# Layer 0 of a four-layer network: products of two slots together in even slots, two convolution taps together in odd slots

## The chip, the cores and the metric

The kernel runs on one core of one Trainium2 chip. The metric is the time of the device in microseconds for one launch, all four layers included. A core has five engines that work side by side and wait for each other through semaphores: PE (TensorE: matrix products and transposes), DVE (VectorE), ACT (ScalarE), POOL (GpSimd) and SP (SyncE, which here issues most DMAs). PEld is PE's weight load, which can overlap its products.

## The reference, cut to what matters

Each of four layers adds the output of one block to `x`, an array of 4 images of 64 x 64 tokens with 128 channels in float32. The change touches layer 0 alone, a selective scan in four directions over the tokens:

```python
xz = x @ in_proj_w.T
xh, z = jnp.split(xz, 2, axis=-1)
z = silu(z)
xc = silu(depthwise_conv_3x3(xh) + conv_b)          # 256 channels
xs = stack([x0, x1, x0[..., ::-1], x1[..., ::-1]])  # rows, columns, and both backwards
dts, Bm, Cm = split(einsum(xs, x_proj_weight))
delta = softplus(dts @ dt_projs_weight + bias)
h = exp(delta * A) * h + (delta * u) * B            # for each of 16 states n, token by token
y = einsum('bkdn,bkn->bkd', h, C)                   # sum over the 16 states
y = layernorm(sum_over_directions(y + Ds * xs)) * z
return y @ out_proj_w.T
```

Here `u` is the input of one direction. The scan over `h` runs along 4096 tokens for 256 channels, 16 states, 4 directions and 4 images.

## The kernel before, in words

**Units and slots.** Layer 0 walks through 128 units: an image `b` (4), a direction `k` (4) and a chunk `c` of 512 tokens (8). A unit has 16 slots `n`, one for each state; there are 2048 slots. The order of instructions on PE, ACT, DVE and POOL is written out by hand: each engine executes in the order in which the loop emits.

**One slot.** POOL multiplies `dB = du * B` (L684). For each half `s` of the channels ACT computes `dA = exp(delta * A)` into a PSUM bank (L689, three banks in turn) and DVE runs the scan `h` (L690) over 512 tokens. The states of four slots form a group `G` of one tile `h`. Some slots later (`LAG`, and the place in a queue) `transposed()` takes a quarter of a group: PE transposes eight 128 x 128 blocks into `pt` (L538; one buffer of two PSUM banks), and ACT copies `pt` to the tile `hT` (L548).

**Products.** `products()` multiplies a copied `hT` with `W`, a sparse arrangement of C that sums over the states, into the PSUM tiles `yT` (L573): four products with 32 output rows each in every slot, which the profile shows as eight records. In a direction `k == 0` four products with the diagonal `D_diag` (L562) stand ahead of them. When a group is the last of its unit, `yT` is added to `y`, and the result is stored. `products()` is called in the slot after that in which its `hT` was copied: after the transposes of that slot, before the slot's side work.

**Side work.** Generators, wrapped in `Side`, give out the work for other images in pieces, each with a kind: `l` (loads), `m`, `n`, `x`, `z` (gates), `f`, `g` and `c` (a tap of the convolution). A piece may be placed in the slots that `SIDE` lists for its kind, and `due()` paces the pieces evenly by their number. A convolution is nine taps (L159), each a product of 128 x 128 weights with 512 tokens that PE makes in two records, added up in one PSUM bank `cv`. Its first tap is placed at `n == 11`; then the property `inside` makes the loop give a tap in each of the next eight slots, so it ends at `n == 3` of the next unit. The bank `m`, of which there is one, is shared by all side work and by the projections of the next unit: `xd_ps` at n=6, `dp` (L465) at n=7 and n=9. `limited` (L474) is DVE's clamp of `delta`, which reads `dp` at n=9 and n=11. After a convolution ACT and DVE compute silu (`e`, in three steps at ACT) and ACT copies it by columns (`xw`, L369).

The side work after an image (`after`) normalises `y`, transposes it, writes it scaled to `yg`, multiplies `yg` by the gates on POOL (L411) and projects it on PE.

There are 52 convolutions in the slots: 20 while image 0 is scanned, 16 each with images 1 and 2, none with image 3.

Of the kernel before, what the change touches and what calls it, by code (L numbers as in the profile page):

```python
# [11 lines left out]
F32 = mybir.dt.float32  # L12
# [70 lines left out]
def layer0(sh, A, x_in, x_out, scr, ahead):  # L83
# [7 lines left out]
    with ExitStack() as ctx:  # L91
# [60 lines left out]
        def conv(xn, s, bank):  # L152

            for t in range(9):
                yield "c"
                if t == 0:
                    pm = bank("cv")
                dy, dx = divmod(t, 3)
                nc.tensor.matmul(  # L159
                    pm,  # L160
                    lhsT=taps[:, s, t, :],
                    rhs=xn[:, dy : dy + 8, dx : dx + 64],
                    start=(t == 0),
                    stop=(t == 8),
                )
            return pm
# [207 lines left out]
        def after(b, st, later, bands):  # L374

            for c in bands:
                yield "l"
                rows = slice(c * CH, (c + 1) * CH)
                if kept:
                    y = kept.pop()  # L380
                else:
                    y = tmp.tile([P, 4, 2 * P], F32, name="yf", tag="t4", bufs=4)
                    nc.sync.dma_start(y, tiles(scr(f"y2{b % 2}")[rows, :]))
                z = tmp.tile([P, 2, CH], F32, name="zf", tag="t4", bufs=4)
                nc.sync.dma_start(z, scr(f"z{b % 3}")[:, :, rows].rearrange("s p t -> p s t"))
                mv = small.tile([P, 4, 2], F32, name="ln_mv")
                for q in range(4):
                    nc.vector.bn_aggr(mv[:, q, :], st[:, 4 * c + q])

                rs = small.tile([P, 4], F32, name="ln_r")  # L390
                later("act1", nc.scalar.activation, rs, mv[:, :, 1], AF.Ln, bias=sh.eps5)
                yield "n"

                nb = spare("nb")[:, 0:4]
                nc.scalar.activation(nb, rs, AF.Exp, scale=-0.5)
                for q in range(4):
                    later("dve", normed, y[:, q, :], mv[:, q, 0:1], nb[:, q : q + 1])
                yg = tmp.tile([P, 2, CH], F32, name="yg", bufs=2)
                for s in range(2):
                    yield "m"  # L400
                    pt = spare("pg")
                    for q in range(4):
                        nc.tensor.transpose(pt[:, q * P : (q + 1) * P], y[:, q, s * P : (s + 1) * P], sh.ident)
                    norm = dict(scale=on_w[:, s : s + 1], bias=on_b[:, s : s + 1])
                    later("act0", nc.scalar.activation, yg[:, s, :], pt, AF.Identity, **norm)
                yield "f"
                xr = tmp.tile([P, 4, DM], F32, name="xr", tag="t2", bufs=4)
                nc.sync.dma_start(xr, tiles(x_in(b)[rows, :]))
                if b < NB - 1:
                    yield "g"  # L410
                nc.gpsimd.tensor_tensor(yg, yg, z, ALU.mult)  # L411
                yield "m"
                op = spare("op").rearrange("p (q d) -> p q d", q=4)
                for q in range(4):
                    for s in range(2):
                        nc.tensor.matmul(
                            op[:, q, :], lhsT=yg[:, s, q * P : (q + 1) * P], rhs=w_out[:, s, :], start=(s == 0), stop=(s == 1)
                        )
                later("dve", residual, b, rows, xr, op, slots=2)
# [100 lines left out]

        LAG = 7
        queue = []
        copied = None

        def transposed():

            nonlocal copied
            todo, copied = copied, None
            pt = None
            if queue:  # L530
                G = queue[0]
                q = G["q"]
                G["q"] += 1
                pt = ps.tile([P, 4, 2, P], F32, name="pt")
                for j in range(4):
                    t0 = q * P + j * 32
                    for s in range(2):
                        nc.tensor.transpose(  # L538
                            pt[:, j, s, :], G["h"][:, s, t0 : t0 + 32, :].rearrange("p t n -> p (t n)"), sh.ident
                        )  # L540
                if q == 3:
                    queue.pop(0)
            if todo is not None:
                products(*todo)
            if pt is not None:
                hT = tmp.tile([P, 4, 2 * P], F32, name="hT")
                copied = G, q, hT
                return lambda: nc.scalar.copy(hT, pt.rearrange("p j s d -> p j (s d)"))  # L548
            return lambda: None

        def products(G, q, hT):
            U = G["unit"]
            rev = U["rev"]
            qo = 3 - q if rev else q
            e = qo // 2
            if U["yT"][e] is None:
                U["yT"][e] = psy.tile([P, 2, 2 * P], F32, name=f"yT{e}")
                if U["k"] == 0:
                    for r in range(2):
                        for s in range(2):  # L560
                            t0 = (2 * e + r) * P
                            nc.tensor.matmul(  # L562
                                U["yT"][e][:, r, s * P : (s + 1) * P],
                                lhsT=U["u"][:, s, t0 : t0 + P],
                                rhs=D_diag[:, s, :],
                                start=(r == 0 and s == 0),
                                stop=False,
                                skip_group_check=True,
                            )
                    U["started"] |= {(e, j) for j in range(4)}  # L570
            for j in range(4):
                jo = 3 - j if rev else j
                nc.tensor.matmul(  # L573
                    U["yT"][e][32 * jo : 32 * jo + 32, qo % 2, :],
                    lhsT=U["Ws"][G["g"]][:, :, 4 * q + j],
                    rhs=hT[:, j, :],
                    start=((e, jo) not in U["started"]),
                    stop=(G["g"] == 3),
                    skip_group_check=True,
                )  # L580
                U["started"].add((e, jo))
            if G["g"] == 3 and q % 2:

                y, k = U["y"], U["k"]
                ye = y[:, 2 * e : 2 * e + 2, :]
                if U["pos"] == 0:
                    (nc.vector.tensor_copy if q == 3 else nc.scalar.copy)(ye, U["yT"][e])
                else:
                    nc.vector.tensor_tensor(ye, ye, U["yT"][e], ALU.add)
                if k == 2:  # L590
                    for r in range(2):
                        nc.vector.bn_stats(U["st"][:, 4 * U["pc"] + 2 * e + r, 0, :], y[:, 2 * e + r, :])
                if q == 3 and U["last"]:
                    kept.append(y)
                elif q == 3:
                    nc.sync.dma_start(U["dst"](k), y)
# [45 lines left out]
        with tc.manual_schedule(engines=order):  # L642
            idle = lambda: None
            left = opening(any_bank, [idle, fetched, idle, begun, grown_steps, readied])
            u, ready, bd, Wd, Bb = (got[n] for n in ("u", "ready", "bd", "Wd", "Bb"))
            sides.append(Side(rest(left, spare, later), 18 * len(left), 0, 2 * NS * len(left)))
            for i, (b, k, c) in enumerate(units):
                if i % per == 0:
                    ln_st = small.tile([P, NJ, 1, 6], F32, name="ln_st")
                    first = len(left) if b == 0 else 0  # L650
                    if b + 1 < NB:
                        sides.insert(len(sides) if b == 0 else 0, Side(before(b + 1, spare, later), 17 + 8 * 22, NS * (i + first), (28 - first) * NS))
                rev = k >= 2
                pos = orders[b].index(k)
                pc = NCH - 1 - c if rev else c
# [16 lines left out]
                for n in range(NS):  # L672
# [14 lines left out]
                    for s in range(2):  # L687
# [4 lines left out]
                        )  # L692
                        steps(n, f"act{s}")
                        flush(f"act{s}")
                    copy = transposed() if slot >= LAG else (lambda: None)
                    copy()
                    steps(n, "act2")
                    flush("act2")
# [26 lines left out]

                    inside = [d for d in sides if d.inside]
                    free = not inside and slot >= taken
                    for d in inside or [d for d in sides if free and n in SIDE[d.need] and d.due(slot)][:1]:
                        taken = slot + SPACE[d.need]
                        d.free_at = slot + 1  # L730
                        d.step()
# [40 lines left out]
class Side:  # L772
# [7 lines left out]
    @property  # L780
    def inside(self):

        return self.need == "c" and self.run % 9 > 0

    def due(self, slot):
        wait = self.need == "l" and self.loads and slot < self.loads[0]
# [1404 lines left out]
```

## Time and profile before

| | |
|---|---|
| time, median of 3 runs | 7696.86 us (7693.64 to 7699.71) |
| the profiled execution | 7694.64 us, span 7692.9 us |
| slots of layer 0 | from 112.8 to 5645.7 us of the span |
| busy over the whole span | PE 82%, DVE 88%, ACT 79%, POOL 74% |
| mean granted TensorE clock | 0.965 of full speed |

The profile shows one execution. Times are microseconds from the start of the span unless marked ns. A group's row gives line, engine, operation, the tiles written and read, the shapes and how often it ran, then the time it kept its engine busy, the mean ns of one, and the engine's idle time just before it with what ended most of it. Rows of a timeline give start, duration, engine, line and operation, with equal neighbours merged ("x8"). PE's records overlap their neighbours, so distances there are read from start to start. "pt(n)", "hT(n)" and so on stand for the instruction of that name in slot n.

### The profile page before, as it was taken

How to read it: one execution, taken by the hardware profiler on the slowest of the kernel's cores; microseconds unless marked ns; L12 is line 12 of the kernel's file. 1: busy time of each engine (PE TensorE's matmuls, PEld its weight loads, DVE VectorE, ACT ScalarE, POOL GpSimd, SP SyncE). 2: the span in 40 equal slices, each digit the busy share in tenths (PEclk: the TensorE clock that was granted, in tenths of full speed). 3: DMA queues.
4: the chain of work that ended last, by engine and by line, in shares of the span. 5: the costliest groups of instructions: out<-in, count | busy, mean ns of one | idle time of the engine just before them, and what ended most of it. 6: DMA issues, size and time to landing. Idle time of an engine off the chain costs nothing.

```text
span 7692.9 us, 140985 instructions
## 1 busy us (share of the span) xinstructions
PE 6324.7 (82%) x52796; PEld 3997.2 (52%) x52796; DVE 6751.7 (88%) x8113; ACT 6094.9 (79%) x9683; POOL 5694.2 (74%) x2718
## 2 busy tenths in 40 slices
PE   7888888888889877888887777787789978676789
PEld 3544444444455544445554444454467756564566
DVE  7999999999999999999999999999966655656678
ACT  7999999999999999999999999999843323314667
POOL 4999999999999999999999999999930024123233
PEclk8999999999999999999999999999999978788899
DMA  6555556555656655465565445555532241231332
GB/s 173 171 169 177 176 171 180 168 172 166 189 174 182 189 188 171 155 183 184 174 193 185 166 168 180 176 182 180 176 107 67 63 115 52 77 103 41 103 97 81
DMA packets 1325856, 1158.87 MB, mean 151 GB/s; under 512 B 694134, under 2 KB 1119698, under 8 KB 1258227
## 3 DMA queue, kind: packets, MB, share of 16 engines
q1 hardware_dynamic: 1320898, 1147.43, 48.7%
q8 instruction: 416, 6.82, 0.4%
q10 hardware_dynamic: 4272, 2.43, 0.1%
q14 instruction: 270, 2.20, 0.1%
HBM read 956.37 MB, written 189.21 MB: 149 GB/s over the span
## 4 chain that ended last, share of the span: by engine, by line
PE 34%; ACT 31%; DVE 19%; issue 8%; POOL 4%; DMA 2%; SPq 1%; ACTq 0%; DVEq 0%; POOLq 0%
ACT hT L548 12%; DVE h L690 12%; ACT dA L689 12%; PE pt L538 7%; PE cv L159 5%; PE yT L573 4%; POOL dB L684 3%; ACT e L631 2%; PE pf L917 2%; PE po L930 1%; ACT delta L468 1%; PE pt L1870 1%; PE pu L1161 1%; PE pa L1161 1%; PE pb L1161 1%
## 5 line engine op out<-in xcount | busy, mean ns | idle before, releaser
L690 DVE TENSOR_TENSOR_SCAN h<-dA,state,dB 128x512 f32<-128x512 f32 x4096 | 4921.4, 1268 | 127.0 <-POOL dB L684 48.0
L684 POOL TENSOR_TENSOR dB<-du,Bb 128x1024 f32<-128x1024 f32 x2048 | 4816.6, 2391 | 162.2 <-DVE h L690 121.9
L538 PE MATMUL pt<-ident,h 128*128 128x128 f32 x16384 | 2221.1, 279 | 824.8 <-ACT hT L548 809.6
L689 ACT ACTIVATE dA<-delta,A_neg 128x512 f32<-128x512 f32 x4096 | 2750.0, 695 | 118.3 <-DVE h L690 95.8
L538 PEld LDWEIGHTS pt<-ident,h 128*128 128x128 f32 x16384 | 1810.0, 142 | 1866.0 <-ACT hT L548 1642.5
L548 ACT COPY hT<-pt 128x1024 f32<-128x1024 f32 x2048 | 2077.2, 1014 | 178.6 <-PE pt L538 158.6
L573 PE MATMUL yT<-hT,W 128*32 128x256 f32 x16384 | 1380.2, 409 | 0.3
L573 PEld LDWEIGHTS yT<-hT,W 128*32 128x32 f32 x16384 | 455.8, 150 | 342.6 <-issue 330.2
L159 PE MATMUL cv<-xn,taps 128*128 128x512 f32 x936 | 526.9, 644 | 2.9 <-DVE delta L474 2.9
L1161 POOL TENSOR_TENSOR xg<-xg,so 128x1024 f32<-128x1024 f32 x16 | 39.3, 2467 | 620.0 <-PE pu L1161 619.4
L1908 POOL TENSOR_TENSOR S<-S,sm 128x784 f32<-128x784 f32 x128 | 191.4, 1495 | 414.6 <-DVE sm L1906 243.1
L477 POOL TENSOR_TENSOR du<-delta,u 128x512 f32<-128x512 f32 x256 | 329.2, 1286 | 188.7 <-DVE delta L474 172.3
L465 PE MATMUL dp<-xd,w_dt 65*128 65x512 f32 x512 | 288.7, 646 | 65.7 <-ACT Ct L456 43.8
L448 PE MATMUL xd_ps<-u,w_x 128*48 128x512 f32 x512 | 249.4, 610 | 18.8 <-DVE e L358 17.6
L1915 ACT ACTIVATE S<-S,mx 128x196 f32<-128x196 f32 x512 | 228.0, 449 | 32.2 <-DVE mx L1942 29.8
L159 PEld LDWEIGHTS cv<-xn,taps 128*128 128x128 f32 x936 | 139.2, 188 | 180.6 <-issue 163.2
L918 ACT ACTIVATE h<-pf,b 128x512 f32<-128x512 f32 x128 | 87.7, 687 | 118.8 <-PE pf L917 100.7
L474 DVE SCALAR_TENSOR_TENSOR delta<-delta,dp 128x512 f32<-128x512 f32 x256 | 171.2, 669 | 3.9 <-ACT delta L471 0.8
L1161 POOL TENSOR_TENSOR WX<-wr,Xs 128x544 f32<-128x544 f32 x40 | 60.7, 1517 | 152.2 <-issue 62.9
L1870 PE MATMUL pt<-ident,S 128*98 128x128 f32 x1024 | 166.3, 287 | 3.4 <-POOL S L1908 2.0
L1161 DVE TENSOR_TENSOR WX<-wr,Xs 128x544 f32<-128x544 f32 x88 | 74.1, 860 | 104.4 <-PE pz L1161 59.5
L465 PEld LDWEIGHTS dp<-xd,w_dt 65*128 65x128 f32 x512 | 76.5, 188 | 170.7 <-ACT Ct L456 97.4
(377 smaller groups left out, 7101.9 us busy)
## 6 DMA issues: line engine op xcount, KB each, us to landing
Bb<-l_B SPq DMA_DIRECT2D x512, 1024.0 KB
W<-l_W SPq DMA_DIRECT2D x512, 256.0 KB
l_y<-y SPq DMA_DIRECT2D x127, 512.0 KB
u<-l_xr SPq DMA_DIRECT2D x64, 512.0 KB
u<-l_xw SPq DMA_DIRECT2D x64, 512.0 KB
y<-l_y SPq DMA_DIRECT2D x56, 512.0 KB
V<-l_v SPq DMA_DIRECT2D x512, 49.0 KB
y<-l_y SPq DMA_DIRECT2D x80, 256.0 KB
```

Of the source, the lines that this page charges most:

```text
L159: nc.tensor.matmul(pm, lhsT=taps[:, s, t, :], rhs=xn[:, dy : dy + 8, dx : dx + 64], start=(t == 0), stop=(t == 8),)
L448: nc.tensor.matmul(bank["x"], lhsT=w_x[:, s, k, :], rhs=u[:, s, :], start=(s == 0), stop=(s == 1))
L465: nc.tensor.matmul(bank[s], lhsT=w_dt[:, k, s * P : (s + 1) * P], rhs=xd, start=True, stop=True)
L477: nc.gpsimd.tensor_tensor(du[:, s, :], delta[:, s, :], u[:, s, :], ALU.mult)
L538: nc.tensor.transpose(pt[:, j, s, :], G["h"][:, s, t0 : t0 + 32, :].rearrange("p t n -> p (t n)"), sh.ident)
L548: return lambda: nc.scalar.copy(hT, pt.rearrange("p j s d -> p j (s d)"))
L573: nc.tensor.matmul(U["yT"][e][32 * jo : 32 * jo + 32, qo % 2, :], lhsT=U["Ws"][G["g"]][:, :, 4 * q + j], rhs=hT[:, j, :], start=((e, jo) n ...
L684: nc.gpsimd.tensor_tensor(dB, du, B_now[:, q : q + 1, :].to_broadcast([P, 2, CH]), ALU.mult)
L689: nc.scalar.activation(dA, delta[:, s, :], AF.Exp, scale=A_neg[:, k, s, n : n + 1])
L690: nc.vector.tensor_tensor_scan(h[:, s, :, q], dA, dB[:, s, :], state[:, s, n : n + 1], ALU.mult, ALU.add)
L1161: r = f(*args, **kw)
L1870: nc.tensor.transpose(pt[:, half, hp, :], U["S"][:, e, hp, 98 * half : 98 * half + 98], sh.ident)
```

## The change

Taps go in pairs, and products in even slots:

- `conv` asks for a new piece only before every second tap, so a convolution is five pieces: taps 0 and 1, 2 and 3, 4 and 5, 6 and 7, and 8. Inside a convolution the loop gives a piece only in slots with odd `n`: 11, 13, 15, 1, 3.
- In slots n = 1, 3, 11, 13 and 15 `transposed(hold=True)` calls no products; the `hT` that are waiting are kept in a list, and the next slot makes the products of both. This is so in every unit, with or without a convolution.
- `hT` gets three buffers instead of two, and `yg` one instead of two; each buffer is 4 KB per partition.
- The numbers of pieces by which side work is paced become 10 instead of 18, and 14 instead of 22.

```diff
         def conv(xn, s, bank):
             for t in range(9):
-                yield "c"
+                if t % 2 == 0:
+                    yield "c"
                 if t == 0:
                     pm = bank("cv")
...
-                yg = tmp.tile([P, 2, CH], F32, name="yg", bufs=2)
+                yg = tmp.tile([P, 2, CH], F32, name="yg", bufs=1)
...
-        copied = None
-
-        def transposed():
-
-            nonlocal copied
-            todo, copied = copied, None
+        copied = []
+
+        def transposed(hold=False):
+
+            todo, copied[:] = copied[:], []
             pt = None
             if queue:
...
-            if todo is not None:
-                products(*todo)
+            if hold:
+                copied[:] = todo
+            else:
+                for each in todo:
+                    products(*each)
             if pt is not None:
-                hT = tmp.tile([P, 4, 2 * P], F32, name="hT")
-                copied = G, q, hT
+                hT = tmp.tile([P, 4, 2 * P], F32, name="hT", bufs=3)
+                copied.append((G, q, hT))
                 return lambda: nc.scalar.copy(hT, pt.rearrange("p j s d -> p j (s d)"))
...
-            sides.append(Side(rest(left, spare, later), 18 * len(left), 0, 2 * NS * len(left)))
+            sides.append(Side(rest(left, spare, later), 10 * len(left), 0, 2 * NS * len(left)))
...
-                        sides.insert(len(sides) if b == 0 else 0, Side(before(b + 1, spare, later), 17 + 8 * 22, NS * (i + first), (28 - first) * NS))
+                        sides.insert(len(sides) if b == 0 else 0, Side(before(b + 1, spare, later), 17 + 8 * 14, NS * (i + first), (28 - first) * NS))
...
-                    copy = transposed() if slot >= LAG else (lambda: None)
+                    copy = transposed(n in {1, 3, 11, 13, 15}) if slot >= LAG else (lambda: None)
...
-                    for d in inside or [d for d in sides if free and n in SIDE[d.need] and d.due(slot)][:1]:
+                    for d in [d for d in inside if n % 2] or [d for d in sides if free and n in SIDE[d.need] and d.due(slot)][:1]:
...
-        return self.need == "c" and self.run % 9 > 0
+        return self.need == "c" and self.run % 5 > 0
```

## The prediction

> **What bounds the kernel now.** I read the page first, then layer 0 alone (a row of the windows view), then DVE's waits, then the order of time inside one unit.
>
> ```profile
> span 7692.9 us, 140985 instructions
> L690 DVE TENSOR_TENSOR_SCAN h<-dA,state,dB 128x512 f32<-128x512 f32 x4096 | 4921.4, 1268 | 127.0 <-POOL dB L684 48.0
> ```
>
> ```profile
> 112.00:5646.00 5534.00, 4572.09 (x36175) 2704.32 (x36176) 5388.46 (x5178) 5165.13 (x7415) 5188.49 (x2375) 0.99 0.56 176
> ```
>
> The columns are PE, PEld, DVE, ACT, POOL. In the 5534 us of layer 0's slots DVE is busy 5388: it bounds them, and the scans are 4921.4/2048 = 2.40 us of each slot. The change adds and removes nothing on DVE, so it can win at most the 145 us in which DVE idles. Adding up DVE's idle gaps by slot number, 43.5 us fall in slot n=5 of the 128 units, and 42.0 of these in the 52 units in which a convolution has just ended: about 0.83 us each in 49 of them, 0.37 to 0.42 in three. One such unit, in its order of time (slots 2 to 5; start, duration, engine, line):
>
> ```profile
> 2421.88 1.04 PE L538 MATMUL pt<-ident,h 128*128 128x128 f32 x8
> 2422.84 0.67 PE L573 MATMUL yT<-hT,W 128*32 128x256 f32 x8
> 2423.01 1.01 ACT L548 COPY hT<-pt 128x1024 f32<-128x1024 f32 x1 [0.31 <-PE pt L538]
> 2423.44 1.13 PE L159 MATMUL cv<-xn,taps 128*128 128x512 f32 x2
> 2424.41 1.04 PE L538 MATMUL pt<-ident,h 128*128 128x128 f32 x8
> ...
> 2429.75 0.70 ACT L689 ACTIVATE dA<-delta,A_neg 128x512 f32<-128x512 f32 x1
> ...
> 2430.55 1.30 DVE L690 TENSOR_TENSOR_SCAN h<-dA,state,dB 128x512 f32<-128x512 f32 x1 [0.82 <-ACT dA L689]
> ```
>
> Start to start, PE spends 0.96 on eight transposes, 0.60 on the products, 0.97 on a tap: 2.53 a slot, more than DVE's 2.40. So in the nine tap slots PE leads: ACT's copy hT waits 0.31 for pt, the next dA stands behind that copy, and DVE's lead is used up (at n=3 the scan starts 0.10 after its dA in 49 of 52 cases). At n=4 ACT has two pieces of silu besides, and DVE waits at n=5.
>
> Without a tap PE does not lead:
>
> ```profile
> 728.22 1.09 PE L538 MATMUL pt<-ident,h 128*128 128x128 f32 x8 [0.97 <-ACT hT L548]
> 729.25 0.67 PE L573 MATMUL yT<-hT,W 128*32 128x256 f32 x8
> 730.47 1.09 PE L538 MATMUL pt<-ident,h 128*128 128x128 f32 x8 [0.56 <-ACT hT L548]
> ```
>
> pt has one buffer, so a slot is the round trip pt, hT, pt: 2.25 here. Where the weights were loaded ahead it is 1.12 (2424.41 to the copy at 2425.53) + 1.01 copy + 0.06 = 2.20.
>
> **What the skill's pages say.** "TensorEngine Tiling (Array Packing)", Key Properties, says that a change of tiling mode drains TensorE, not a change of tile. The products use 128x32 tiles, transposes and taps the whole array. The trace agrees and prices it:
>
> ```profile
> 2401.35 1.09 PE L538 MATMUL pt<-ident,h 128*128 128x128 f32 x8
> 2402.28 1.06 PE L562 MATMUL yT<-D_diag,u 128*128 128x128 f32 x8
> ```
>
> ```profile
> 40.60 7.89 PE L159 MATMUL yT<-xn,taps 128*128 128x512 f32 x18
> 48.38 1.12 PE L240 MATMUL pv<-h,w_in 128*128 128x512 f32 x2
> ```
>
> pt to another whole-array group takes 0.93 (2401.35 to 2402.28), where pt to the products takes 1.03 (728.22 to 729.25), both with weights not loaded ahead. Nine taps in a row take 7.78, 0.86 each, against 0.97 behind products. A switch is thus about 0.1 us. "Perfetto Trace Analysis", Per-engine timelines, says that TensorE's end times are estimated; the merged PE rows do overlap (1.04 long, next start after 0.96). I go by starts.
>
> **The change part by part.**
>
> 1. Tap slots. A convolution still starts at n=11 and ends at n=3, but its taps stand two at a time in slots 11, 13, 15, 1 and one in 3, where no products run; products of two slots stand together in 12, 14, 0, 2, 4. Odd slot: 0.93 + 2 x 0.86 = 2.65. Even slot: 0.96 + 0.60 for the first products + 0.43 to 0.60 for the second (0.43 is two sets of four concurrent 256-column products at the 0.109 by which single 128-column transposes start apart; 0.60 is the first again) = 1.99 to 2.16. That is under the round trip, so an even slot takes 2.20. A pair takes 4.85 instead of 2 x 2.53 = 5.06: 0.21 saved, three pairs (13 to 2), 0.63 per convolution. The single tap of slot 3 stands behind pt(3), so it does not count.
>
> 2. Start of the convolution. Its first tap needs the PSUM bank that DVE's clamp of delta (L474) still reads at n=11. Today products stand before the tap and cover that wait:
>
> ```profile
> 2403.98 1.09 PE L538 MATMUL pt<-ident,h 128*128 128x128 f32 x8
> 2404.81 0.66 DVE L474 SCALAR_TENSOR_TENSOR delta<-delta,dp 128x512 f32<-128x512 f32 x1
> ...
> 2405.60 0.30 PEld L159 LDWEIGHTS cv<-xn,taps 128*128 128x128 f32 x2 [0.38 <-DVE delta L474]
> ```
>
> Without them PE is ready at 2404.92, waits to 2405.53, and the two taps (0.53 + 3 x 0.43 = 1.82) hold pt(12) to 2407.35. Queued behind are pt(12), hT(12), dA(13): hT(12) starts at 2408.48 instead of 2407.83, pt(13) at 2409.55 instead of 2409.24: +0.31. Then -0.63, and +0.06 because the next hT comes 1.18 after a pt whose weights were not loaded ahead: -0.26. The same for all 52 by their own wait: 29 waits near 0.37 give +0.09 and -0.48; 13 near 0.60 give -0.26; 10 of 0.94 or more give +0.53 and about -0.08. Sum: 13.9 + 3.4 + 0.8 = 18.1 us earlier. It reaches DVE, since the scan at n=5 waits for the dA behind these copies, and 0.83 of idle is more than 0.48; dB is ready 0.56 us or more before that scan, so POOL does not take it back.
>
> 3. Products held in slots without taps. The doubled slot needs 1.03 to 1.20 after pt, the hold slot nothing; the 0.56 of idle before pt (728 to 731) covers the added 0.43 to 0.60. Without that cover ACT still has 0.15 a slot against DVE's 2.40. Products at n=5 to 10, which release y and its store, stay.
>
> 4. Side work. In a doubled slot a gate or transposition comes 0.43 to 0.60 later. Of 48 gates, 14 at n=12 mostly wait for xn anyway and 14 at n=14 meet an ACT busy with silu; 12 at n=0, 2, 4 may cost up to 0.5 each: at most 6, I take 1.5 us. The pacing counts 14 pieces per chunk instead of 22, so loads, gates and convolutions of images 1 and 2 move by up to a unit; all still end inside their image, with the same number of convolutions.
>
> 5. Buffers. The third hT is needed because two are held while a third is written; its earlier products stand before pt in PE's order, so the copy waits for nothing new. One yg instead of two: the next write reads transposes that stand behind the last reader in PE's order; nothing. Products one slot later free W one slot later: SP, which already waits 242 us for that (120 times), waits up to a slot longer, with the state copy, the Bb, u and y loads behind it. W is issued 15 us or more before use and Bb mostly 14, and the state copy waits for DVE anyway: nothing; POOL's waits for Bb are 7 us now.
>
> Sum: -18.1 + 1.5 = -16.6 us. The profiled execution took 7694.6 us (span 7692.9), so 7678; the median of the runs is 2.2 higher: 7680.
>
> **Rivals.**
>
> - No change (7697, 7690 to 7702): the wait at n=5 is ACT's own, made by the silu at n=4. Against it: ACT has no gap from n=4 on and hangs on hT(3), which PE sets; for it: few of these waits are long.
> - Slower: the doubled products outlast the round trip. Place: slots 12, 14, 0, 2. If all four sets take 0.33 (half the merged 0.67), the slot is 0.96 + 1.32, with 0.1 of weight load exposed 2.38; the pair is 5.03 and saves 0.09 in three. The start costs 0.23 on average (29 x 0.09, 13 x 0.31, 10 x 0.53 over 52) plus 0.06: +0.20 x 52 = 10 us, and the 40 gates in doubled slots at 0.35 cost 14: 7697 + 24 = 7721. It decides where a pair exceeds 5.06 - 0.29/3 = 4.96. Against it: in the single records the two sets of a slot's products start 0.27 apart.
> - Larger gain: ACT and DVE are early enough at n=11 for the clamp to be done when pt(11) ends, so that the start costs nothing and all of 52 x 0.63 = 33 us stays, which DVE's 42 us at n=5 would still admit: 7662 to 7664. For it: shifted convolutions meet other work at n=9 to 11. Against it: every one of the 52 waits is over 0.2 now.
> - The change not doing what it says: the new order has 260 tap slots instead of 468 and runs of eight product instructions (16 records), so this gets no chance.
>
> **Numbers.** Forecast 0.60 (own range 7670 to 7692), larger gain 0.10, no change 0.14, slower 0.16. A difference under 0.2%, 15.4 us, can't be told from none here. The forecast sits at that edge: 0.37 of its 0.60 lies beyond. Faster 0.37 + 0.10 = 0.47; same 0.23 + 0.14 = 0.37; slower 0.16. The range runs from 7660, past the larger gain, to 7708, which takes in the slower case where only half of its cost comes; some 0.1 is left out above and little below.
>
> **What would show it.** After: pt starts 2.65 and 2.20 apart in tap slots; the gap before hT there gone in even slots; DVE's idle at n=5 down from 42 to some 24 us; pt(12) 0.5 to 0.8 later against pt(11), with the taps' weight load waiting for delta (L474); scans still 1.2 each. Wrong: even slots over 2.3, DVE's idle at n=5 unchanged, or new DVE idle at n=12 to 2.

## The result, and the profile after

The changed kernel takes **7706.51 us** (median of 20 runs, 7699.29 to 7717.29), the kernel before 7694.64 in the same comparison (20 runs, 7687.76 to 7703.18). The ratio is 1.0016, with a 95% interval of 1.0009 to 1.0022: about 12 us slower, where 16.6 us less was forecast. By the bound of 0.2% this is still "no change"; the interval says that it is a small loss, not none. The median lies 26.5 us above the forecast, near the top of the range.

The page and layer 0 in the windows view (columns PE, PEld, DVE, ACT, POOL, then the granted clock, DMA share, GB/s):

```profile
span 7709.7 us, 140598 instructions
L693 DVE TENSOR_TENSOR_SCAN h<-dA,state,dB 128x512 f32<-128x512 f32 x4096 | 4918.1, 1270 | 133.3 <-ACT dA L692 62.2
112.00:5659.00 5547.00, 4468.78 (x36178) 2778.35 (x36179) 5385.71 (x5178) 5160.03 (x7413) 5186.66 (x2375) 0.98 0.55 176
```

Layer 0 is 13 us longer (5547 against 5534), with the same scans and nearly the same busy time of DVE (5385.7 against 5388.5). The wait of the scan for `dA` grew from 43.0 (in the full list of the scan's waits before) to 62.2 us. One more number moved: the mean clock of TensorE in layer 0, from 0.99 to 0.98.

**Inside the convolutions the forecast came true.** PE in one of them (rows of the timeline for PE alone, slots 13 to 15):

```profile
2110.39 1.09 PE L538 MATMUL pt<-ident,h 128*128 128x128 f32 x8
2111.32 1.88 PE L160 MATMUL cv<-xn,taps 128*128 128x512 f32 x4
2113.04 1.04 PE L538 MATMUL pt<-ident,h 128*128 128x128 f32 x8
2114.00 1.10 PE L576 MATMUL yT<-hT,W 128*32 128x256 f32 x16
2115.24 1.09 PE L538 MATMUL pt<-ident,h 128*128 128x128 f32 x8
```

`pt` to `pt`: 2.65 in the odd slot, 2.20 in the even one. Over all 52 convolutions the medians are:

| pt(n) to pt(n+1), us | n=11 | 12 | 13 | 14 | 15 | 0 | 1 | 2 | 3 | 4 |
|---|---|---|---|---|---|---|---|---|---|---|
| before | 2.66 | 2.59 | 2.53 | 2.53 | 2.53 | 2.53 | 2.53 | 2.53 | 2.53 | 2.97 |
| after | 3.20 | 2.15 | 2.65 | 2.20 | 2.65 | 2.20 | 2.65 | 2.20 | 2.25 | 3.23 |

From the scan of n=10 to that of n=7 of the next unit (start to start) a convolution took 34.33 us before (mean of 52) and 34.01 after: 0.33 less, 17.0 us for the 52. So 30 us were lost elsewhere.

**Where they were lost.** Image 3 has no convolution, and still its 32 units took 1355.8 us before and 1358.7 after. Eighteen of the units agree within 0.1 us, eleven lose 0.1 to 0.9, and three take 0.5 to 0.8 less (two of these come straight after a unit that lost; in the third the kernel before runs at half speed). Unit 4, counted from 0, takes 41.46 us against 40.64. Three neighbouring stretches of 3.41 us in it (windows view of the changed kernel, columns as above):

```profile
4464.38:4467.79 3.41, 3.11 (x32) 1.99 (x30) 3.41 (x6) 2.11 (x3) 3.41 (x3) 1.00 0.77 258
4467.79:4471.20 3.41, 1.38 (x16) 1.16 (x20) 3.41 (x4) 3.07 (x5) 3.41 (x2) 1.00 0.83 284
4471.20:4474.61 3.41, 3.30 (x24) 1.85 (x16) 3.41 (x4) 2.57 (x4) 3.41 (x3) 0.50 0.57 205
```

In the second PE is busy 1.38 of 3.41 us: its products are held back in slot 1, which is long here (3.87 us from `pt` to `pt`; 3.92 before). The kernel before, in the stretch that lies at the same distance from its `pt(1)`, is busy 1.77 us:

```profile
4456.84:4460.25 3.41, 1.77 (x20) 1.28 (x18) 3.41 (x4) 3.02 (x5) 3.41 (x2) 1.00 0.90 305
```

In the third stretch of the changed kernel the clock granted to TensorE is 0.50. The timeline shows what that does to the chain `pt`, `hT`, `dA`:

```profile
4470.84 1.69 PE L576 MATMUL yT<-hT,W 128*32 128x256 f32 x16
...
4472.63 1.97 PE L538 MATMUL pt<-ident,h 128*128 128x128 f32 x8
4474.69 1.01 ACT L551 COPY hT<-pt 128x1024 f32<-128x1024 f32 x1 [0.92 <-PE pt L538]
```

The doubled products take 1.69 instead of 1.10 and the transposes 1.97 instead of 1.09, just where twice the products stand before them. The clock records that begin in the layer-0 slots hold 13 such half-speed stretches before and 39 after, each 3.41 us or twice that. That is the first theory. The second is the pacing: in images 1 and 2, 30 of the 32 convolutions start a unit or two later than before, and GpSimd's waits for a load of Bb rose from 7.1 us (one wait) to 23.5 (six).

### The profile page after: what moved, and what is told of

The parts are those of the page before. It is cut to its first block, busy times and chain, and to the rows that moved or that the text cites. A ratio compares the mean times of both kernels' runs of the same rounds, so it can differ in the third digit from the quotient of the medians.

```text
span 7709.7 us, 140598 instructions
## 1 busy us (share of the span) xinstructions
PE 6225.9 (81%) x52796; PEld 4073.3 (53%) x52796; DVE 6752.0 (88%) x8113; ACT 6089.5 (79%) x9683; POOL 5689.3 (74%) x2718
## 4 chain that ended last, share of the span: by engine, by line
ACT 33%; PE 31%; DVE 20%; issue 8%; DMA 3%; POOL 3%; SPq 1%; ACTq 0%; DVEq 0%; POOLq 0%
ACT hT L551 14%; DVE h L693 12%; ACT dA L692 12%; PE pt L538 7%; PE cv L160 5%; POOL dB L687 2%; ACT e L634 2%; PE pf L920 2%; PE po L933 1%; PE yT L576 1%; PE pu L1164 1%; PE pz L1164 1%; PE pt L1873 1%; ACT delta L469 1%; PE pa L1164 1%
## 5 line engine op out<-in xcount | busy, mean ns | idle before, releaser
L693 DVE TENSOR_TENSOR_SCAN h<-dA,state,dB 128x512 f32<-128x512 f32 x4096 | 4918.1, 1270 | 133.3 <-ACT dA L692 62.2
L576 PE MATMUL yT<-hT,W 128*32 128x256 f32 x16384 | 1243.7, 405 | 0.7
L576 PEld LDWEIGHTS yT<-hT,W 128*32 128x32 f32 x16384 | 518.0, 148 | 316.1 <-issue 236.4
L160 PE MATMUL cv<-xn,taps 128*128 128x512 f32 x936 | 452.9, 602 | 22.3 <-DVE delta L475 22.1
L160 PEld LDWEIGHTS cv<-xn,taps 128*128 128x128 f32 x936 | 157.4, 190 | 135.2 <-issue 110.2
L472 ACT ACTIVATE delta<-delta 128x512 f32<-128x512 f32 x256 | 164.9, 645 | 0.0
```

The costliest lines, as they stand in the source:

```text
L160: nc.tensor.matmul(pm, lhsT=taps[:, s, t, :], rhs=xn[:, dy : dy + 8, dx : dx + 64], start=(t == 0), stop=(t == 8),)
L576: nc.tensor.matmul(U["yT"][e][32 * jo : 32 * jo + 32, qo % 2, :], lhsT=U["Ws"][G["g"]][:, :, 4 * q + j], rhs=hT[:, j, :], start=((e, jo) n ...
L693: nc.vector.tensor_tensor_scan(h[:, s, :, q], dA, dB[:, s, :], state[:, s, n : n + 1], ALU.mult, ALU.add)
```

## The experiments

Each row is a kernel; "half-speed" counts the half-speed records that begin in the layer-0 slots of its one profile (most last 3.41 us, some two or three times that; in B, C, F, K, L and M one of 27 us at the start of layer 0 is among them), "low windows" is explained below the table. The first two times are from the first comparison; the runs of the kernel before beside the others had medians of 7694.26, 7693.90 and 7694.98 us.

| kernel | us, median | ratio to before (95%) | half-speed | low windows |
|---|---|---|---|---|
| before | 7694.64 | | 13 | 14 |
| changed | 7706.51 | 1.0016 (1.0009 to 1.0022) | 39 | 43 |
| A old pacing | 7704.21 | 1.0015 (1.0008 to 1.0021) | 37 | 43 |
| B old pacing, held in convolutions only | 7680.63 | 0.9981 (0.9973 to 0.9989) | 15 | 14 |
| C as A, zero products in the empty slots | 7673.37 | 0.9974 (0.9965 to 0.9984) | 6 | 12 |
| D as C, a quarter of the columns | 7681.00 | 0.9982 (0.9976 to 0.9989) | 21 | 19 |
| E held in convolutions only, own pacing | 7681.40 | 0.9984 (0.9977 to 0.9990) | 15 | 17 |
| F as B, first tap alone | **7646.32** | 0.9935 (0.9922 to 0.9947) | 14 | 16 |
| G as F, held everywhere | 7662.68 | 0.9963 (0.9950 to 0.9977) | 30 | 38 |
| H as F, own pacing | 7654.63 | 0.9950 (0.9938 to 0.9963) | 15 | 17 |
| K before, with the new pacing | 7708.43 | 1.0018 (1.0012 to 1.0025) | 8 | 17 |
| L held, taps single | 7761.60 | 1.0090 (1.0076 to 1.0104) | 32 | 43 |
| M taps in pairs, nothing held | 7809.14 | 1.0150 (1.0136 to 1.0164) | 13 | 15 |

**A: the changed kernel with the pacing of before.**

```diff
-            sides.append(Side(rest(left, spare, later), 10 * len(left), 0, 2 * NS * len(left)))
+            sides.append(Side(rest(left, spare, later), 18 * len(left), 0, 2 * NS * len(left)))
...
-        self.done += 1
+        self.done += 2 if self.need == "c" and self.run < 4 else 1
```

(and 22 for 14 in the other count)

> The changed kernel, but the side work is counted as before: 18 and 22 pieces for each convolution, a slot with two taps counting as two pieces, so that a convolution starts in the same units as in the kernel before. Theory 1 (the clock): the added time comes from half-speed stretches of TensorE's clock after the slots that are left without products; the pacing doesn't matter: about 7706 us, as the changed kernel, with about 39 half-speed stretches in the slots of the first layer. Theory 2 (the pacing): the added time comes from side work that is moved later in images 1 and 2, and from the loads of Bb behind it: about 7695 us, as the kernel before, or less, and GpSimd's wait for the load of Bb falls from 23.5 us to about 7. Both at work, as the budget of the traces has it (37 us to explain, 8 to 11 of them in images 1 and 2): 7695 to 7700 us.

7704.21 us: 2.3 less than the changed kernel, where the runs of each spread over 18 us. Theory 2 alone falls; by this run the pacing has little to do with the loss, and the half-speed stretches stay. But A restores the counts and not the places: in the traces 38 of its 52 convolutions begin in the unit in which they begin before, and 14 one or two units earlier. B, C, D and M have A's places, E, H and K exactly those of the changed kernel, L those of the kernel before; in F and G, 14 convolutions begin a unit later than before. So the comparisons on the clock (A with B, C and D; changed with E; F with G) are between kernels with the same places, and those on the pacing are not all with the places of before.

**B: held only where a convolution is under way.**

```diff
+                    within = any(d.inside for d in sides)
+                    if not within and slot >= taken and n == 11:
+                        within = any(d.need == "c" for d in [d for d in sides if n in SIDE[d.need] and d.due(slot)][:1])
-                    copy = transposed(n in {1, 3, 11, 13, 15}) if slot >= LAG else (lambda: None)
+                    copy = transposed(within and n in {1, 3, 11, 13, 15}) if slot >= LAG else (lambda: None)
```

> As the kernel with the old pacing, and products are held back in slots 1, 3, 11, 13 and 15 only where a convolution is under way; elsewhere they come one slot after their transposes, as in the kernel before. Theory 1 (the clock): the half-speed stretches of image 3 and of the units without taps go (from 39 to about 15 in all), some 10 to 15 us less than the kernel with the old pacing: about 7685 us. Theory 2 (the pacing alone): held products in slots without taps cost nothing: the same time as the kernel with the old pacing, within 3 us. Rival: held products gain something of their own in the slots without taps: 3 us or more slower.

7680.63 us, 23.6 less than A, with 15 stretches for 37; the layer-0 slots are 25.0 us shorter in the profiles, 6 to 7 in each image, and the convolutions themselves are as in A (34.00 us for 33.94). So it is the holding in slots outside a convolution that costs. It doesn't say yet that the clock is the reason.

**C: the same held products, but TensorE kept busy.**

```diff
+        none = wp.tile([P, 32], F32, name="none")
+        nc.vector.memset(none, 0.0)
...
+                nc.tensor.matmul(
+                    U["yT"][qo // 2][32 * jo : 32 * jo + 32, qo % 2, :],
+                    lhsT=none,
+                    rhs=hT[:, j, :],
+                    start=False,
...
             if hold:
                 copied[:] = todo
+                if fill:
+                    for each in todo:
+                        nothing(*each)
```

> As the changed kernel with the old pacing (products held in slots 1, 3, 11, 13 and 15 everywhere), but in these slots, where no convolution is under way, TensorE is given as many products as it had there in the kernel before: the copied transposes times zeros, added to the sums of the slot, which changes no value. The held products are still done two slots' worth together one slot later. Theory 1 (the clock: TensorE has too little to do in the slots without products, and drops to half speed for 3.4 us): the half-speed stretches fall from 40 to about 15, and the time by some 20 us, to about 7684 us, as where products are held only within convolutions. Rival (the doubled products themselves come too late in slots without taps): no less than the changed kernel with the old pacing, 7704 us or more, since TensorE only gets more to do.

7673.37 us: TensorE does 3024 more product records than in A, and the kernel is 30.8 us faster. Held and doubled products cost nothing that shows once the slot that they leave is not empty. Layer 0 of A and of C in the windows view:

```profile
112.00:5650.00 5538.00, 4470.51 (x36180) 2780.75 (x36180) 5384.52 (x5178) 5163.20 (x7415) 5188.82 (x2375) 0.98 0.56 176
```

```profile
112.00:5627.00 5515.00, 4635.17 (x39202) 2817.04 (x39202) 5379.89 (x5178) 5162.65 (x7416) 5188.58 (x2375) 1.00 0.56 177
```

PE is busy 165 us more, its clock is 1.00 instead of 0.98, and the stretch is 23 us shorter. The rest of the 30.8 lies outside layer 0, which varied by up to 19 us between profiles (2042.9 to 2061.5 us from the last scan of layer 0 to the end). The same holds for the 11 us by which C beats its expectation and the 7 by which it beats B: in the profiles its layer 0 is as long as B's (5515 and 5513), and no run here says where they come from.

**What decides a stretch.** In every profile the half-speed stretches begin on a grid of 3.413 us, at another place of the program in each. So I cut the layer-0 slots along that grid and took PE's busy share in each window from its records, leaving out windows that were at half speed themselves:

| PE busy in a window (13 profiles) | windows | next one at half speed |
|---|---|---|
| under 0.455 | 181 | 181 |
| 0.455 to 0.55 | 972 | 76 |
| over 0.55 | 19512 | 1 |

"Low windows" in the large table counts windows under 0.46 for every possible position of the grid, divided by the number of positions: what one should expect whatever the phase. It runs from 12 to 43 over the kernels. The four that hold products in every unit and fill nothing (changed, A, G, L) have 38 to 43 and also the most stretches, D with its small filler lies next in both, and the others have 12 to 17; among these the order of the two columns differs (K has 17 low windows and 8 stretches). The Trainium skill ("TensorE: Matmul & The Clock Gate", Part 1: The HAM clock gate) states a free-running window of 3413 ns and a clock that is half or full, lower after an idle window. The trace agrees on all of this; it adds that half speed came after every window in which TensorE was busy under 0.455 of it. Between 0.455 and 0.55 it came after one in thirteen, and what decides there stays open.

**D: the rule put to the test.** The zero products with 64 of 256 columns:

```diff
-                    U["yT"][qo // 2][32 * jo : 32 * jo + 32, qo % 2, :],
+                    U["yT"][qo // 2][32 * jo : 32 * jo + 32, qo % 2, 0:64],
...
-                    rhs=hT[:, j, :],
+                    rhs=hT[:, j, 0:64],
```

> As the kernel with products with zeros in the slots left without any, but with 64 of the 256 columns: some 0.1 us of TensorE's time in place of 0.4. Ten profiles so far show TensorE's half-speed stretches on a grid of 3.41 us: a window in which TensorE was busy under 0.46 of the time by the records was always followed by one, a window over 0.55 all but never. Theory (the clock, decided by the busy share of a window): with 0.1 us more in each such slot, the number of windows under 0.46 in the profile with the old pacing, at any position of the grid, falls from 43 to 22 (with 0.4 us: to 15), so two thirds to three quarters of the gain of the full filler: 7680 to 7684 us. Rival (what counts is that some product is there at all, or the whole work of a slot): 7673 us as with the full filler, or 7704 us as without.

7681.00 us, 21 stretches, 19 low windows: inside what the rule gave for the time. In D the zero products add 71 us to PE's busy time in layer 0 (4541.97 against 4470.51), 0.19 us in each of the 378 slots by the records. "Always" in the expectation was too much for its 0.46: in the ten profiles then at hand, 54 windows lie between 0.455 and 0.46, and half speed came after 29 of them. Therefore the table has its line at 0.455. In the three profiles that came after the expectation (D, H and M) the windows under 0.455 were followed by half speed in 37 of 37 cases, those over 0.55 in none of 4554.

**K and E: what the pacing costs.** K is the kernel before with the counts 10 and 14, and `self.done += 5 / 9 if self.need == "c" else 1`; E is the changed kernel with the edit of B alone.

> The kernel before with nothing changed but the counts by which side work is paced: a convolution counts 5 pieces instead of 9 (and 10 and 14 instead of 18 and 22 for each), as in the changed kernel, so that convolutions start in the changed kernel's units. Theory 1 (the clock alone): no change, 7695 us. Theory 2 (the pacing): 8 to 11 us slower than the kernel before, 7703 to 7706 us, with GpSimd's wait for the load of Bb up from 7 us to about 23.

> The changed kernel, and products are held back only where a convolution is under way; the pacing is the changed kernel's own. With the kernel with the old pacing, with and without products held elsewhere, this makes a square of two by two. If the two costs add up: the pacing costs what it did in the kernel before (14 us), so 7681 + 14 = 7695 us. If the pacing costs nothing in the changed kernel (2 us between the changed kernel and that with the old pacing): 7681 to 7684 us.

K takes 7708.43 us, 14.2 more than before, with fewer half-speed stretches: the pacing does cost, by another way. E takes 7681.40, 0.8 more than B. In all four pairs (with H and F below) the layer-0 slots of the profile are longer with the new pacing, by 8.4 (K), 10.0 (changed against A), 12.1 (E) and 10.0 us (H), most of it in image 1, and in images 1 and 2 of each of these four kernels GpSimd waits three times over 3 us for Bb. One such place in the changed kernel (timeline; SPq is SP's queue):

```profile
1825.68 0.32 SPq L360 DMA_DIRECT2D l_xr<-e  x1
1826.05 0.43 SPq L329 DMA_DIRECT2D xt<-in_x  x1
1829.05 0.55 SPq L371 DMA_DIRECT2D l_xw<-xw  x1
1830.04 4.21 SPq L453 DMA_DIRECT2D l_B<-xd  x1
1834.35 2.13 SPq L462 DMA_DIRECT2D l_W<-Ct  x4
1836.57 0.39 SPq L599 DMA_DIRECT2D l_y<-y  x1
1837.23 1.29 SPq L489 DMA_DIRECT2D Bb<-l_B  x2
...
1842.94 2.38 POOL L687 TENSOR_TENSOR dB<-du,Bb 128x1024 f32<-128x1024 f32 x1 [3.66 <-DMA Bb<-l_B]
...
1845.35 2.46 DVE L693 TENSOR_TENSOR_SCAN h<-dA,state,dB 128x512 f32<-128x512 f32 x2 [2.10 <-POOL dB L687]
```

The same unit of the kernel before:

```profile
1831.08 0.33 SPq L452 DMA_DIRECT2D l_B<-xd  x1
1831.69 1.64 SPq L461 DMA_DIRECT2D l_W<-Ct  x4
1833.43 0.39 SPq L596 DMA_DIRECT2D l_y<-y  x1
1833.92 2.37 SPq L488 DMA_DIRECT2D Bb<-l_B  x2
```

A convolution now ends just there, so its stores of `e` and `xw` stand in SP's queue before the store of B; the issue of that one takes 4.21 us instead of 0.33, the first Bb goes out 3.3 us later, and the scan stands 2.10 us. The long issue is nothing new in itself. In every kernel it comes once after each convolution, in 52 of the 128 units; for instance in the kernel before:

```profile
2005.90 4.20 SPq L452 DMA_DIRECT2D l_B<-xd  x1
```

New is the place. All 17 waits of over 3 us for Bb in images 1 and 2 of the thirteen profiles come at the end of unit 39, 55, 71 or 87, when a convolution has ended in it: each is the last unit of a direction whose successor runs backwards. With the new pacing convolutions end in all four of these units, in the kernel before, F, G and L in none, and in A to D and M in 55 and 87 (where A, B and M wait once, D twice, C not at all). So the end of a convolution there is needed for the wait but does not always bring it; why it brings it at some of these ends and not at others stays open. Three waits at the 2.10 us above would be some 6 of the 8 to 12 us, an estimate from that one place. The medians follow only in part: 14.2 and 8.3 us (K, H), but 2.3 and 0.8 (changed, E). The one wait that A and B have themselves (4.6 and 5.1 us, near 3931 and 3910 us) narrows the gap. Why the medians of these two pairs show so little stays open.

**F, G and H: the first tap alone.**

```diff
-                if t % 2 == 0:
+                if t == 0 or t % 2:
                     yield "c"
...
+                    copy = transposed(within and n in {1, 3, 13, 15}) if slot >= LAG else (lambda: None)
```

F is B with this, and with `self.done += 2` for the four pairs instead of the first four pieces: one tap in slot 11, where products run, and pairs in 13, 15, 1 and 3. G holds in those four slots of all units; H is F with the changed kernel's own pacing.

> As the kernel that holds products only within convolutions with the old pacing, but the first tap goes alone into slot 11 (where no products are held), and the other eight in pairs into slots 13, 15, 1 and 3. If the forecast's sum was right in its steps on the slots (0.63 us saved for each convolution over three pairs of slots, none lost at the start where two taps wait for the clamp's delta), the 52 convolutions of the first layer give 52 x 0.63 = 33 us less than the kernel before: about 7662 us. If the first pair's wait for delta is no loss, the same as the kernel that pairs from slot 11: within 3 us of it. If VectorE's scan sets the time within convolutions too, as elsewhere: no less than 7685 us.

> As the kernel with the first tap alone in slot 11 and the old pacing, but products are held in slots 1, 3, 13 and 15 everywhere, with a convolution or without. By the theory of the clock the stretches at half speed come back (30 or more in place of 11) and cost about what they do with the first pair at slot 11, where four slots in five hold: 15 to 24 us more, 7661 to 7670 us. By the rival that it was holding in slot 11 alone that cost: 7646 us as without.

> The changed kernel with its own pacing, with the first tap alone in slot 11 and products held only where a convolution is under way and in slots 1, 3, 13 and 15: the third pair for the pacing. If the pacing costs what it does in the kernel before (14 us): 7660 us. If it costs what it did in the two other pairs of changed kernels (1 to 2 us): 7647 us.

F takes 7646.32 us, 48 less than the kernel before and 16 better than the best expectation, which had carried over three pairs: with the first tap alone the ninth tap has a partner, and it is four. A convolution takes 33.51 us (mean), 0.82 less than before, where 4 x 0.21 = 0.84 is the sum; against B, with the pair at slot 11, it is 0.49 less. `pt(11)` to `pt(13)` takes 4.89 us in the mean in place of B's 5.43: so much does the wait for delta cost the pair at slot 11. In the slots 12 to 1 the scans now start 2.35 us apart in the median: DVE sets the pace. Layer 0 of F:

```profile
112.00:5601.00 5489.00, 4500.14 (x36173) 2718.55 (x36172) 5365.44 (x5178) 5167.41 (x7417) 5187.24 (x2375) 0.99 0.56 177
```

G, 16.4 us more and 30 stretches for 14, is the clock's price once more, within what was expected. H costs 8.3 us more than F, between the two values.

**L and M: each half of the change alone** (old pacing). L holds as the changed kernel does and leaves the taps single; M pairs the taps and holds nothing (`copy = transposed()`).

> Products held back as in the changed kernel, in all units, but the taps one to a slot as in the kernel before, old pacing. What the slots cost by the sum of the forecast: an odd slot 0.93 + 0.86 = 1.79 us, which VectorE's 2.35 covers, an even slot 2.20 + 0.86 = 3.06: 5.41 us a pair against 5.06 before where TensorE sets both, so 4 pairs x 0.35 x 52 = 73 us slower at most; where VectorE covers the odd slot and TensorE catches up in it, the same work of TensorE as in the changed kernel, 4.85 a pair, and about the changed kernel's time, 7704 us. By the clock's theory the half-speed stretches of the units without taps stay at about 30.

> Taps in pairs as in the changed kernel, but products in every slot, none held; old pacing. The other half of the change alone. By the forecast's sum an odd slot is 0.93 + 1.27 + 2 x 0.86 less what overlaps, 3.38 us, and an even one VectorE's 2.35: 5.73 us a pair, against 5.06 before: 4 pairs x 0.67 x 52 = 139 us slower at most; if TensorE works ahead in the even slots as it did where products were held with single taps (5.13 to 5.21 us a pair where 5.41 was computed), some 5.3 to 5.5: 50 to 90 us slower, 7745 to 7785 us. Half-speed stretches as in the kernel before (about 13).

L takes 67.7 us more than the kernel before beside it (7693.90). Its even slots are 3.02 us from `pt` to `pt`, as computed, but its odd ones 2.19, not 1.79: I had forgotten that the round trip bounds these too. The convolutions, 35.20 us for 34.33, account for 45 us; the clock (43 low windows, as A) is at hand for the rest, which no run separates. M takes 114 us more: 3.45 + 2.19 = 5.64 a pair, and 4 x (5.64 - 5.06) x 52 = 121. TensorE does not work ahead in its even slots. Neither half gains alone; together a pair is 4.85.

## Why the prediction was wrong, point by point

1. **Tap slots: right.** 2.65 and 2.20 were computed and measured. The rival in which the doubled products outlast the round trip is out.
2. **Start of the convolution: right.** pt(11) to pt(13) was to be 0.23 us later on average over the 52; the means are 3.39 + 2.15 against 2.71 + 2.58, 0.25 later. The two steps together gave 18.1 us in the forecast (17.7 if its third group is summed from its own terms: 0.53 + 0.06 - 0.63 is -0.04, not -0.08); the convolutions of the changed kernel are 17.0 us shorter, and B, the change without its losses elsewhere, is 13.6 us faster than before. The path of the gain was not as told, though. DVE's idle at n=5 fell only from 42.0 to 34.9 us in these units, not to 24: the gain showed up earlier, in slots 15 to 3, where the scans start 12.10 us apart in all instead of 12.63 (medians). And most of the idle at n=5 does not hang on PE: in F, whose scans follow at DVE's pace in slots 12 to 1, it is still 36.2 us, and ACT is busy 5.39 of the 5.49 us from the scan of n=3 to that of n=5 (mean of the 52). On this wait the rival "no change" read the trace better.
3. **"The hold slot nothing": the step that failed.** It looked at the length of the doubled slot and at its cover, and took a slot with less work as free. Where such a slot leaves a window of 3.41 us less than 0.455 busy, it costs TensorE half its clock for the next 3.41 us, and doubled products and transposes, which then set the pace, fall into them. The forecast put it at nothing; it cost 23.6 to 25.1 us. Filling the slots again gives back 30.8 us (A to C), emptying fewer 23.6 (A to B) and 25.1 (changed to E). None of the forecast's signs of being wrong could show this, as all of them lie inside convolutions: even slots took 2.20, and DVE's idle in n=12 to 2 was 13.2 us before and 12.6 after. The trace of before held the answer: if its products of slots 1, 3, 11, 13 and 15 are moved behind those of the next slot, on paper, its low windows go from 14 to 41; the changed kernel has 43. At the 23.6/(43 - 14) = 0.8 us each that A and B show this is 22 us.
4. **Side work: the pacing at nothing was wrong too.** The place is the one named in step 5, Bb's loads behind others in SP's queue; "mostly 14" us of lead left out the exceptions, and moving convolutions put their stores into units 39, 55, 71 and 87, where Bb then came too late. The difference in the medians is 0.8 to 14 us by pair; in this kernel, against A, it is 2.3, which is within the scatter.
5. **The sum.** 7694.3 - 13.6 (before to B) + 23.6 (B to A, holding elsewhere) + 2.3 (A to changed, pacing) = 7706.6. These are the steps from run to run, so that they meet the measured 7706.5 proves nothing; they say how large each part is. The forecast's 7680 is B's time, partly by luck: B gains 13.6 us, not 16.6, and the forecast set out from a median that was 2.2 us higher than that of the 20 runs.
6. **The bound of 145 us, DVE's idle time**, was too low as a ceiling. In F layer 0 is shorter by 45 us, of which 23 are DVE's recorded busy time (5388.46 to 5365.44) with the same instructions: scans that follow at once overlap in the records, by 86 ns in the median before and 89 in F, and a wait that only shortens the overlap counts as busy time. The durations of DVE's instructions one by one sum to no less in F (5797 us against 5784).

## What to carry to other kernels

Moving work of TensorE into bursts empties the slots in between, and in this kernel a slot that was emptied was not free: count its busy share over windows as long as the clock's (here 3.41 us), at every position, in the old trace with the work moved on paper. Batch only where something else fills the gap, or fill it; here zero products that keep PE busy 0.19 us more in each empty slot were worth 23 us. And when taps go in pairs, start with the odd one where a wait stands in front of the first.

## What the runs showed of the hardware

Half speed came after windows in which TensorE was far from idle: under 0.455 busy was enough in every one of 181 cases, and over 0.55 was safe but for one case in 19512. Apart from the start of layer 0, PE never stood idle for longer than 3.04 us at a time there in the changed kernel, and it has 39 half-speed stretches. Each low window more cost some 0.8 to 1 us of this kernel (23.6 us for 29 from A to B, 30.8 for 31 from A to C, the latter in part outside layer 0). That is less than the 1.7 us of work that TensorE loses in 3.41 us at half speed; a likely reason is that part of it falls where TensorE is not on the path, which no run here shows.
